# A convolution-attention kernel in float32: another way through the last pair of heads, and another order of the first loads

## The chip, the cores and the metric

The kernel runs on one core of one Trainium2 chip. The metric is the device time of one execution in microseconds (us); a profile of one execution is taken beside the timed runs. Two kinds of number are used: medians of timed runs, and moments in the profiled execution, counted from its start. In lines of a profile PE is TensorE, PEld its weight loads, DVE VectorE, ACT ScalarE, POOL GpSimd and SP SyncE, which issues most transfers; a q behind a name is that engine's queue of instructions.

## The reference, cut to what matters

Four images of 384 channels and 48 x 48 pixels go through one block: a 7 x 7 depthwise convolution is layer-normed and added to the queries of an 8-head self-attention over the 2304 pixels, followed by a projection and a residual.

```python
local = conv(x, conv_w, groups=C) * inv + (bn_beta - bn_mean * inv)     # 7x7, depthwise
x_norm = layernorm(x_flat, ln_gamma, ln_beta)
q, k, v = split(x_norm @ qkv_w.T + qkv_b)                               # 8 heads of 48
q = q + heads(layernorm(local_flat, ln_gamma, ln_beta))
attn = softmax(q @ k.T * 48 ** -0.5)
out = x_flat + (attn @ v) @ proj_w.T + proj_b
```

## The kernel before

The work is cut into 24 tiles (`t`) of 384 pixels (8 image rows); each tile goes through four pairs of heads. The sums of a pair, `pt` times `v`, carry a column of ones, so the softmax denominators arrive as row 48 of each head. Up to pair 2 a pair fills one 128-row chunk of `ao` (rows 0 to 47 and 64 to 111); the 96 rows of pair 3 are cut in six pieces that fill the gaps. The denominators go through DRAM to be inverted by 128 lanes and broadcast back. The end of the program, for the last tile:

```python
def pair_end(t, p):                       # cut
    for j in range(2):
        r = 64 * j
        nc.scalar.copy(dst[r : r + HA], sums[r : r + HA, :G])
        nc.sync.dma_start(out=den[2 * p + j : 2 * p + j + 1], in_=dst[r + HD : r + HA])
    if p == NP - 1:                       # six pieces of pair 3 into the gaps of ao
        ...

def divide(t):                            # cut
    nc.sync.dma_start(out=rd, in_=den)    # 8 x 384 sums on 128 lanes, 24 each
    nc.vector.reciprocal(rd, rd)
    nc.sync.dma_start(out=rden, in_=rd)
    # every reciprocal is checked against a safe range; the result goes into `inside`
    ...                                   # four broadcasts of rden into rb
    return rb

weigh()                                   # the last sums
load_residual(NT - 1)
rb = divide(NT - 1)
ao = outputs[NT - 1][0]
nc.vector.tensor_mul(ao, ao, rb)
for co in range(CC):
    output_step(NT - 1, co)               # project 3 chunks, add bias and residual, store
# then: count the lanes outside the range -> flag -> every engine loads the flag and
# branches: nothing more to do, or a second pass with shifted exponents
```

The start, before the first tile's scores (about 148 us), convolves the first tile partly on TensorE (the first `PE_TAPS` taps, as products with diagonal matrices that ScalarE makes) and partly on VectorE, norms the six pieces of the first image in turn ("cycles"), and folds the norm's beta into the projections' biases: three rows computed on TensorE (`row`) go to DRAM (`bias`) and come back as columns (`columns`, then `qkb`), because the kernel adds a bias as one value to a lane.

```python
load_slab(0, 0)                           # SP queue: image rows for the first convolution
...                                       # 14 vector pieces, in turn on the ACT and the SP queue
load_x(0, 0)
load_packed(w_v, ...)                     # then staged[1], x1, staged[0], x2 to x5, w_o,
...                                       # the second slab and the first residual
```

Of the kernel before, what the change touches and what calls it, by code (L numbers as in the profile page):

```python
# [16 lines left out]
NH = 8  # L17
# [9 lines left out]
OUT_SLOTS = 5, 8, 10  # L27
PE_TAPS = 12

# [13 lines left out]
def unshifted_pass(  # L43
# [94 lines left out]
    nc.sync.dma_start(out=taps_in, in_=conv_w)  # L138
    load_slab(0, 0)
    nc.gpsimd.tensor_scalar_add(inv, norms[:, 3], BN_EPS)  # L140
    nc.gpsimd.tensor_tensor(inv, inv, neg_half, ALU.pow)
# [34 lines left out]
    ]  # L176
    load_x(0, 0)
    load_packed(w_v, qkv_wT[:, 2 * C :])
# [38 lines left out]
    def conv_ops(t):  # L217
# [9 lines left out]
        for tap in taps if t else taps[PE_TAPS:]:  # L227
            for c in range(CC):
# [11 lines left out]
                yield  # L240

    def first_products(dst, c):
        slab, first, end = slabs[0, 0]
        for i, tap in enumerate(taps[:PE_TAPS]):
            n = c * PE_TAPS + i
            diagonal = diagonals[n // 6].rearrange("p i f -> p (i f)")[:, n % 6 * P :][:, :P]
            nc.scalar.mul(diagonal, ident, cw[:, c, tap : tap + 1])
            src, part = window(slab, dst, 0, first, end, c, tap)
            nc.tensor.matmul(
                part, lhsT=diagonal, rhs=src, start=i == 0, stop=i == PE_TAPS - 1  # L250
            )
# [142 lines left out]
    def weights_layout():  # L394
# [11 lines left out]
        for c in range(CC):  # L406
            nc.scalar.mul(w_v[:, c], w_v[:, c], gain[:, c : c + 1])
        for i in (1, 0):
            if i == 0:
                for j, m in enumerate(rows):  # L410
                    nc.scalar.copy(row[0:1, :, j], m)
                nc.sync.dma_start(out=bias.rearrange("(o c) i -> o c i", o=1), in_=row[0:1])
# [57 lines left out]
    def pair_end(t, p):  # L470
# [6 lines left out]
        ao, ao3, den = outputs[t]  # L477
        dst = ao[:, p, :] if p < CC else ao3
        for j in range(2):
            r = 64 * j  # L480
            nc.scalar.copy(dst[r : r + HA], sums[r : r + HA, :G])  # L481
            nc.sync.dma_start(out=den[2 * p + j : 2 * p + j + 1], in_=dst[r + HD : r + HA])
        if p == NP - 1:
            for c in range(CC):
                for r in (0, 64):
                    nc.sync.dma_start(
                        out=ao[r + HD : r + 64, c, :], in_=ao3[r + 16 * c : r + 16 * c + 16]
                    )

    def divide(t):  # L490

        ao, ao3, den = outputs[t]
        few = NH * G // P
        rd = work.tile([P, few], F32, tag="rd", name="rd")
        rden = dram.tile([NH, G], F32, tag="rden", name=f"rden{t}")
        rb = work.tile([P, CC, G], F32, tag="rb", name="rb", bufs=1)
        flat = "h (k f) -> (h k) f"
        nc.sync.dma_start(out=rd, in_=den.rearrange(flat, f=few))
        nc.vector.reciprocal(rd, rd)
        nc.sync.dma_start(out=rden.rearrange(flat, f=few), in_=rd)  # L500

        for bound, op in ((SAFE, ALU.is_le), (1 / SAFE, ALU.is_ge)):
            nc.vector.scalar_tensor_tensor(inside, rd, bound, inside, op, ALU.mult)
        heads = rden[0:6].rearrange("(c h) n -> h c n", h=2)
        for j in range(2):
            r = 64 * j
            nc.sync.dma_start(
                out=rb[r : r + HD], in_=heads[j : j + 1].to_broadcast([HD, CC, G])
            )
            last = rden[6 + j : 7 + j].rearrange("o (x n) -> o x n", x=1)  # L510
            nc.sync.dma_start(out=rb[r + HD : r + 64], in_=last.to_broadcast([16, CC, G]))
        return rb
# [11 lines left out]
    def output_step(t, co):  # L524
        b, g = divmod(t, NG)
        ao, xr = outputs[t][0], residuals[t]
        m = bank()
        project(m[:, :G], lambda c: w_o[:, c, co * P : (co + 1) * P], lambda c: ao[:, c, :])
        nc.vector.scalar_tensor_tensor(  # L529
            xr[:, co, :], m[:, :G], pb[:, co : co + 1], xr[:, co, :], ALU.add, ALU.add  # L530
        )
# [52 lines left out]
    r, r2 = ring(), ring()  # L584
    products = r[:, 0, :G], r[:, 1, :G], r2[:, 0, :G]
    first_products(products[0], 0)
    convolve_first(16)
# [18 lines left out]
    for g in range(NG):  # L606
# [12 lines left out]
        if g == NG - 1:  # L619
            r, r2 = ring(), ring()  # L620
            for u, m in enumerate((r[:, 0], r[:, 1], r2[:, 0])):
                query_step(0, u, m)
        convolve_first(6)
        rs = newton(*root)
# [9 lines left out]
    for t in range(NT):  # L634
# [14 lines left out]
        for s in range(NSLOT):  # L649
            scores(t, s)  # L650

            if s == 2 and t:
                rb = divide(t - 1)
            if s == X_SLOTS[1] + 1 and coming is not None:
                rs = newton(*root)
# [32 lines left out]
            if s == OUT_SLOTS[0] - 1 and t:  # L688
                ao = outputs[t - 1][0]
                nc.vector.tensor_mul(ao, ao, rb)  # L690
            if s == X_SLOTS[0] - 1 and coming is not None:
                total[X_SLOTS[0]] = chunk_sum(coming)
# [4 lines left out]
            if s == first + 1 and following:  # L697
                total[second] = chunk_sum(sq)
    weigh()
    load_residual(NT - 1)  # L700
    rb = divide(NT - 1)
    ao = outputs[NT - 1][0]
    nc.vector.tensor_mul(ao, ao, rb)  # L703
    for co in range(CC):
        output_step(NT - 1, co)

# [527 lines left out]
```

## Time and profile before

The median is 3159.97 us of the first three runs (3156.47 to 3162.11). The profiled span is 3159.7 us. It falls into three stretches:

| stretch | from, to (us) | length |
|---|---|---|
| start: until the first scores | 0 to 147.94 | 147.9 |
| middle: 24 tiles, TensorE never idle | 147.94 to 3127.79 | 2979.9 |
| end: behind the last sums | 3127.79 to 3159.7 | 31.9 |

First, the bias round trip in the timeline of the kernel before (columns: start us, length us, engine, line, operation, destination<-source, count; "SPq" is the queue of SyncE):

```profile
50.93 0.29 SPq L412 DMA_DIRECT2D bias<-row  x1
53.64 1.76 SPq L96 DMA_DIRECT2D columns<-bias  x4
```

The columns can be issued only when the row has landed: 53.64 less 50.93 is 2.7 us. Second, the branch at the end, in the view of its source line (engine, operation, count, shortest/median/longest ns, first and last start):

```profile
L727 POOLq COMPARE_BRANCH  x1: 62/62/62, 3137.1 to 3137.1; - x1
L727 POOLq EVENT_SEMAPHORE  x1: 17/17/17, 3141.0 to 3141.0; - x1
L727 SPq COMPARE_BRANCH  x1: 45/45/45, 3154.9 to 3154.9; - x1
L727 SPq EVENT_SEMAPHORE  x8: 17/17/17, 3157.4 to 3158.0; - x8
```

GpSimd (POOL) branches 18 us before SyncE does, since the flag is ready at 3136.5 and GpSimd has nothing else to do. The branch itself takes 62 ns, but its next instruction starts 3.9 us later; for SyncE it is 2.5 us.

### The profile page before, as it was taken

To read this page: it belongs to the slowest core of one execution; us is meant where nothing else is said; L and a number is where in the kernel's file an instruction comes from. 1 tells how busy PE (TensorE), PEld (TensorE's weight loads), DVE (VectorE), ACT (ScalarE), POOL (GpSimd) and SP (SyncE) were. 2 spreads that over 40 slices of the span, in tenths; PEclk is the share of its full clock that TensorE was granted. 3 is DMA by queue.
4 is the path that set the end of the run, shared out by engine and by line. 5 is a ranking of instruction groups with operands and counts; after the bars stand their busy time and mean duration, and the time that the engine had idled before them with its cause. 6 is when DMAs were issued, how large, how long until landed. Compare 5 with 4: busy or idle time off the path is not lost.

```text
span 3159.7 us, 41999 instructions
## 1 busy us (share of the span) xinstructions
PE 3074.7 (97%) x15854; PEld 1375.8 (44%) x15854; DVE 2189.8 (69%) x4184; ACT 1615.3 (51%) x2395; POOL 13.1 (0%) x49
## 2 busy tenths in 40 slices
PE   7999999999999999999999999999999999999997
PEld 3544444444454444444454444444445444444443
DVE  6899878867717788778681878877757287777310
ACT  4455555555445555555534555555552555555552
POOL 1000000000000000000000000000000000000000
PEclk9999999999999999999999999999999999999998
DMA  6111111011101111111111111012011001100001
GB/s 110 32 22 28 33 24 43 25 28 37 29 23 31 34 32 28 33 30 31 29 36 24 26 30 43 25 24 45 25 20 30 18 25 31 26 22 20 14 25 32
DMA packets 77255, 96.51 MB, mean 31 GB/s; under 512 B 22193, under 2 KB 67825, under 8 KB 77042
## 3 DMA queue, kind: packets, MB, share of 16 engines
q1 hardware_dynamic: 76322, 93.68, 13.1%
q8 instruction: 127, 2.08, 0.3%
q14 instruction: 86, 0.70, 0.1%
q10 hardware_dynamic: 304, 0.04, 0.0%
q0 software_dynamic: 416, 0.01, 0.0%
HBM read 68.22 MB, written 14.75 MB: 26 GB/s over the span
## 4 chain that ended last, share of the span: by engine, by line
PE 90%; ACT 5%; DMA 2%; DVE 1%; issue 1%; SPq 0%; POOL 0%; ACTq 0%; DVEq 0%
PE r L551 36%; PE o L564 35%; PE m L342 10%; PE r L342 7%; PE m L313 3%; ACT pt L555 2%; ACT u L328 1%; ACT y L329 1%; ACT u L330 1%; ACT sq L321 1%; DVE acc L239 0%; ACT ao L481 0%; DMA xn<-in_x_dram 0%; DMA staged<-in_qkv_wT_dram 0%; DVE xn L626 0%
## 5 line engine op out<-in xcount | busy, mean ns | idle before, releaser
L555 ACT ACTIVATE pt<-r 128x768 f32<-128x768 f32 x1728 | 1275.8, 811 | 1161.0 <-PE o L564 889.1
L239 DVE SCALAR_TENSOR_TENSOR acc<-slab,vec,acc 128x360 f32<-128x360 f32 (+3 forms) x3423 | 1733.5, 588 | 8.1 <-POOL acc L225 7.6
L564 PE MATMUL o<-pt,v 128*49 128x384 f32 x6912 | 1175.5, 490 | 0.0
L551 PE MATMUL r<-q,k 48*128 48x384 f32 x5184 | 920.3, 500 | 6.1 <-ACT pt L555 6.1
L564 PEld LDWEIGHTS o<-pt,v 128*49 128x49 f32 x6912 | 426.3, 124 | 710.0 <-issue 710.0
L551 PEld LDWEIGHTS r<-q,k 48*128 48x128 f32 x5184 | 434.0, 185 | 491.1 <-ACT pt L555 251.2
L551 PE MATMUL r<-qt,kt 48*128 48x384 f32 x1728 | 309.1, 499 | 29.7 <-ACT pt L555 29.7
L529 DVE SCALAR_TENSOR_TENSOR xr<-m,pb,xr 128x384 f32<-128x384 f32 x72 | 44.5, 618 | 298.2 <-PE m L342 298.2
L551 PEld LDWEIGHTS r<-qt,kt 48*128 48x128 f32 x1728 | 147.9, 185 | 189.8 <-ACT pt L555 108.7
L317 DVE TENSOR_TENSOR xn<-xn,m 128x1152 f32<-128x1152 f32 x24 | 32.5, 1354 | 254.1 <-PE m L313 254.1
L342 PE MATMUL m<-ao,w_o 128*128 128x384 f32 x432 | 164.7, 519 | 8.6 <-DVE ao L703 7.2
L342 PE MATMUL m<-xn,w_qk 128*128 128x384 f32 x414 | 152.0, 503 | 0.0
L342 PE MATMUL r<-xn,w_qk 128*128 128x384 f32 x450 | 149.3, 486 | 0.7 <-ACT q L454 0.7
L342 PE MATMUL r<-w_v,xn 128*128 128x384 f32 x432 | 145.3, 489 | 0.0
L334 DVE SCALAR_TENSOR_TENSOR u<-m,eps,u 128x384 f32<-128x384 f32 x48 | 29.6, 618 | 130.0 <-ACT u L330 129.8
L342 PEld LDWEIGHTS m<-ao,w_o 128*128 128x128 f32 x432 | 79.0, 196 | 89.9 <-issue 38.1
L342 PEld LDWEIGHTS r<-xn,w_qk 128*128 128x128 f32 x450 | 85.4, 190 | 60.6 <-ACT q L454 1.3
L342 PEld LDWEIGHTS r<-w_v,xn 128*128 128x128 f32 x432 | 82.4, 191 | 59.0 <-issue 3.0
L342 PEld LDWEIGHTS m<-xn,w_qk 128*128 128x128 f32 x414 | 73.0, 189 | 74.2 <-issue 27.8
L481 ACT COPY ao<-o 49x384 f32<-49x384 f32 x144 | 68.3, 474 | 68.7 <-PE o L564 66.9
L313 PE MATMUL m<-sum,mean_w 128*128 128x384 f32 x192 | 88.0, 540 | 10.5 <-DVE sum L307 8.5
L382 ACT COPY v<-r 128x384 f32<-128x384 f32 x72 | 32.2, 482 | 126.8 <-PE r L342 126.8
(78 smaller groups left out, 741.1 us busy)
## 6 DMA issues: line engine op xcount, KB each, us to landing
xr<-in_x_dram SPq DMA_DIRECT2D x24, 576.0 KB
out_dram<-xr SPq DMA_DIRECT2D x72, 192.0 KB
slab<-in_x_dram SPq DMA_DIRECT2D x32, 378.0 KB
xn<-in_x_dram SPq DMA_DIRECT2D x48, 216.0 KB
rb<-rden SPq DMA_DIRECT2D x48, 216.0 KB
slab<-in_x_dram SPq DMA_DIRECT2D x16, 297.0 KB
slab<-in_x_dram SPq DMA_DIRECT2D x32, 126.0 KB
xn<-in_x_dram SPq DMA_DIRECT2D x48, 72.0 KB
```

What stands on the lines that cost most here:

```text
L239: nc.vector.scalar_tensor_tensor(dst, src, weight, dst, ALU.mult, ALU.add)
L313: nc.tensor.matmul(m[:, :G], lhsT=mean_w, rhs=s, start=True, stop=True)
L317: nc.vector.tensor_sub(src, src, over_chunks(m[:, :G]))
L321: nc.scalar.activation(sq, src, AF.Square)
L328: nc.scalar.activation(u, m[:, :G], AF.Ln, bias=eps)
L342: nc.tensor.matmul(dst, lhsT=weights(c), rhs=src(c), start=c == 0, stop=c == CC - 1)
L382: nc.scalar.copy(v[:, u + NB, :, 0:HD], r[:, j, :C].rearrange("p (h d) -> p h d", d=HD))
L481: nc.scalar.copy(dst[r : r + HA], sums[r : r + HA, :G])
L529: nc.vector.scalar_tensor_tensor(xr[:, co, :], m[:, :G], pb[:, co : co + 1], xr[:, co, :], ALU.add, ALU.add)
L551: nc.tensor.matmul(r[:, j, :G], lhsT=kk[:, blk * P : (blk + 1) * P], rhs=qq, start=True, stop=True)
L555: nc.scalar.activation(pt, r[:, :, :G], AF.Exp, scale=SCALE)
L564: nc.tensor.matmul(sums[r : r + HA, :G], lhsT=values[t // NG, kb // NB][:, kb % NB, 2 * p + j, :], rhs=pt[:, j, :], start=kb == 0, stop=kb ...
```

## The change

At the end, six heads of the last tile are divided before the last pair is done; the sums of heads 6 and 7 are spread over their lanes by a small product, inverted where they lie and projected from where they lie with a weight tile of their own, so that nothing of the last pair goes through DRAM on the path. At the start, the first x is loaded ahead of the vectors, all diagonals are made first, two taps move from TensorE to VectorE, and one bias row is copied early.

```diff
-PE_TAPS = 12
+PE_TAPS = 10
     load_slab(0, 0)
+    load_x(0, 0)
 ...                                                   # vectors
-    load_x(0, 0)
     load_packed(w_v, qkv_wT[:, 2 * C :])
 ...
+    make_diagonals()                                  # was: inside first_products, set by set
     first_products(products[0], 0)
 ...
+        nc.scalar.copy(row[0:1, :, 2], rows[2])       # ahead of the scaling of the weights
         for i in (1, 0):
             if i == 0:
-                for j, m in enumerate(rows):
-                    nc.scalar.copy(row[0:1, :, j], m)
+                for j in (1, 0):
+                    nc.scalar.copy(row[0:1, :, j], rows[j])
 ...
-        convolve_first(6)
+        convolve_first(7)
 ...
+            if s == NSLOT - 1 and not following:      # last slot of the last tile
+                load_residual(t)
+                rb = divide(t, 6)                     # heads 0 to 5
 ...
     weigh()
-    load_residual(NT - 1)
-    rb = divide(NT - 1)
-    nc.vector.tensor_mul(ao, ao, rb)
-    for co in range(CC):
-        output_step(NT - 1, co)
+    r, r2 = ring(), ring()
+    parts = r[:, 0, :G], r[:, 1, :G], r2[:, 0, :G]
+    first_six(0)                                      # 3 products of chunk 0, not yet closed
+    m = bank()
+    nc.tensor.matmul(m[:, :G], lhsT=ending[:, 1, 0:P], rhs=ao3, start=True, stop=True)
+    for co in range(1, CC):
+        first_six(co)
+    nc.vector.reciprocal(y, m[:, :G])
+    nc.vector.tensor_mul(ao3, ao3, y)
+    for co in range(CC):
+        nc.tensor.matmul(parts[co], lhsT=ending[:, 0, co * P : (co + 1) * P], rhs=ao3,
+                         start=False, stop=True)
+        finish(NT - 1, co, parts[co])                 # bias, residual, store
+    reciprocals(NT - 1, 6, NH)                        # the check of heads 6 and 7
```

(Cut: the two copies of the last pair on two engines, the fill of `ending`, the memsets.)

More of the change, by code (lines that the diff above doesn't have):

```diff
@@ L240, in conv_ops, with diagonal, make_diagonals @@
                 yield
+    def diagonal(c, i):
+        n = c * PE_TAPS + i
+        return diagonals[n // 6].rearrange("p i f -> p (i f)")[:, n % 6 * P : n % 6 * P + P]
+    def make_diagonals():
+        for c in range(CC):
+            for i, tap in enumerate(taps[:PE_TAPS]):
+                nc.scalar.mul(diagonal(c, i), ident, cw[:, c, tap : tap + 1])
     def first_products(dst, c):
@@ L244, in first_products @@
         for i, tap in enumerate(taps[:PE_TAPS]):
-            n = c * PE_TAPS + i
-            diagonal = diagonals[n // 6].rearrange("p i f -> p (i f)")[:, n % 6 * P :][:, :P]
-            nc.scalar.mul(diagonal, ident, cw[:, c, tap : tap + 1])
             src, part = window(slab, dst, 0, first, end, c, tap)
             nc.tensor.matmul(
-                part, lhsT=diagonal, rhs=src, start=i == 0, stop=i == PE_TAPS - 1
+                part, lhsT=diagonal(c, i), rhs=src, start=i == 0, stop=i == PE_TAPS - 1
             )
@@ L478, in pair_end @@
         dst = ao[:, p, :] if p < CC else ao3
+        final = t == NT - 1
+        if final and p == 0:
+            nc.gpsimd.memset(ao, 0.0)
+            nc.gpsimd.memset(ao3, 0.0)
         for j in range(2):
             r = 64 * j
-            nc.scalar.copy(dst[r : r + HA], sums[r : r + HA, :G])
+            if final and j:
+                nc.vector.tensor_copy(dst[r : r + HA], sums[r : r + HA, :G])
+            else:
+                nc.scalar.copy(dst[r : r + HA], sums[r : r + HA, :G])
             nc.sync.dma_start(out=den[2 * p + j : 2 * p + j + 1], in_=dst[r + HD : r + HA])
-        if p == NP - 1:
+        if p == NP - 1 and not final:
             for c in range(CC):
@@ L488, in pair_end, with reciprocals, divide @@
                     )
-    def divide(t):
-        ao, ao3, den = outputs[t]
+    def reciprocals(t, h0, h1):
         few = NH * G // P
-        rd = work.tile([P, few], F32, tag="rd", name="rd")
-        rden = dram.tile([NH, G], F32, tag="rden", name=f"rden{t}")
-        rb = work.tile([P, CC, G], F32, tag="rb", name="rb", bufs=1)
-        flat = "h (k f) -> (h k) f"
-        nc.sync.dma_start(out=rd, in_=den.rearrange(flat, f=few))
-        nc.vector.reciprocal(rd, rd)
-        nc.sync.dma_start(out=rden.rearrange(flat, f=few), in_=rd)
-        for bound, op in ((SAFE, ALU.is_le), (1 / SAFE, ALU.is_ge)):
-            nc.vector.scalar_tensor_tensor(inside, rd, bound, inside, op, ALU.mult)
+        n = (h1 - h0) * G // few
+        rd = work.tile([P, few], F32, tag="rd", name="rd")[0:n]
+        nc.sync.dma_start(
+            out=rd, in_=outputs[t][2][h0:h1].rearrange("h (k f) -> (h k) f", f=few)
+        )
+        nc.vector.reciprocal(rd, rd)
+        for bound, op in ((SAFE, ALU.is_le), (1 / SAFE, ALU.is_ge)):
+            nc.vector.scalar_tensor_tensor(inside[0:n], rd, bound, inside[0:n], op, ALU.mult)
+        return rd
+    def divide(t, n=NH):
+        rb = work.tile([P, CC, G], F32, tag="rb", name="rb", bufs=1)
+        rden = dram.tile([NH, G], F32, tag="rden", name=f"rden{t}")
+        if n < NH:
+            nc.gpsimd.memset(rb, 0.0)
+        rd = reciprocals(t, 0, n)
+        nc.sync.dma_start(
+            out=rden[0:n].rearrange("h (k f) -> (h k) f", f=NH * G // P), in_=rd
+        )
         heads = rden[0:6].rearrange("(c h) n -> h c n", h=2)
@@ L509, in divide @@
             )
-            last = rden[6 + j : 7 + j].rearrange("o (x n) -> o x n", x=1)
-            nc.sync.dma_start(out=rb[r + HD : r + 64], in_=last.to_broadcast([16, CC, G]))
+            if n == NH:
+                last = rden[6 + j : 7 + j].rearrange("o (x n) -> o x n", x=1)
+                nc.sync.dma_start(out=rb[r + HD : r + 64], in_=last.to_broadcast([16, CC, G]))
         return rb
@@ L524, in output_step, with finish @@
     def output_step(t, co):
-        b, g = divmod(t, NG)
-        ao, xr = outputs[t][0], residuals[t]
+        ao = outputs[t][0]
         m = bank()
         project(m[:, :G], lambda c: w_o[:, c, co * P : (co + 1) * P], lambda c: ao[:, c, :])
+        finish(t, co, m[:, :G])
+    def finish(t, co, m):
+        b, g = divmod(t, NG)
+        xr = residuals[t]
         nc.vector.scalar_tensor_tensor(
-            xr[:, co, :], m[:, :G], pb[:, co : co + 1], xr[:, co, :], ALU.add, ALU.add
+            xr[:, co, :], m, pb[:, co : co + 1], xr[:, co, :], ALU.add, ALU.add
         )
@@ L653, in unshifted_pass @@
                 rb = divide(t - 1)
+            if s == 0 and not following:
+                ending = big.tile([P, CC, G], F32, tag="xn0", name="ending")
+                nc.gpsimd.memset(ending[:, 0, :], 0.0)
+                for j in range(2):
+                    r = 64 * j
+                    nc.sync.dma_start(
+                        out=ending[r : r + HD, 0, :], in_=proj_wT[(6 + j) * HD : (7 + j) * HD]
+                    )
+                    nc.gpsimd.tensor_copy(
+                        ending[:, 1, r : r + 64], ident[:, r + HD : r + HA].to_broadcast([P, 64])
+                    )
+            if s == NSLOT - 1 and not following:
+                load_residual(t)
+                rb = divide(t, 6)
             if s == X_SLOTS[1] + 1 and coming is not None:
@@ L690, in unshifted_pass @@
                 nc.vector.tensor_mul(ao, ao, rb)
+            if s == NSLOT - 1 and not following:
+                ao = outputs[t][0]
+                nc.vector.tensor_mul(ao, ao, rb)
             if s == X_SLOTS[0] - 1 and coming is not None:
@@ L699, in unshifted_pass, with first_six @@
     weigh()
-    load_residual(NT - 1)
-    rb = divide(NT - 1)
-    ao = outputs[NT - 1][0]
-    nc.vector.tensor_mul(ao, ao, rb)
-    for co in range(CC):
-        output_step(NT - 1, co)
+    ao, ao3, _ = outputs[NT - 1]
+    r, r2 = ring(), ring()
+    parts = r[:, 0, :G], r[:, 1, :G], r2[:, 0, :G]
+    def first_six(co):
+        for c in range(CC):
+            nc.tensor.matmul(
+                parts[co],
+                lhsT=w_o[:, c, co * P : (co + 1) * P],
+                rhs=ao[:, c, :],
+                start=c == 0,
+                stop=False,
+            )
+    first_six(0)
[3 more added lines that the diff above has]
+        first_six(co)
+    y = work.tile([P, G], F32, tag="y", name="y", bufs=1)
+    nc.vector.reciprocal(y, m[:, :G])
+    nc.vector.tensor_mul(ao3, ao3, y)
+    for co in range(CC):
+        nc.tensor.matmul(
+            parts[co],
+            lhsT=ending[:, 0, co * P : (co + 1) * P],
+            rhs=ao3,
+            start=False,
+            stop=True,
+        )
+        finish(NT - 1, co, parts[co])
+    reciprocals(NT - 1, 6, NH)
 def conv_attention(tc: tile.TileContext, *args):
```

## The prediction

> **What bounds the kernel now.** I read the page first (busy shares, chain), then the timeline and chain of waits of the last 60 us and the first 150 us, because the listing of both kernels' instruction orders shows that between the first and the last of the 24 tiles nothing moves on any engine.
>
> ```profile
> PE 3074.7 (97%) x15854; PEld 1375.8 (44%) x15854; DVE 2189.8 (69%) x4184; ACT 1615.3 (51%) x2395; POOL 13.1 (0%) x49
> PE 90%; ACT 5%; DMA 2%; DVE 1%; issue 1%; SPq 0%; POOL 0%; ACTq 0%; DVEq 0%
> ```
>
> Busy shares, then the chain by engine: from about 148 us to 3128 us TensorE is never without a matmul, and the change touches none of those. It can only win at the two ends: some 148 us at the start and 32 us at the end. The chain of waits at the end (start us, us, what):
>
> ```profile
> 3119.89 7.90 PE o L564 x48
> 3127.82 0.47 ACT aot L481
> ...
> 3128.32 0.48 ACT aot L481
> ...
> 3132.92 1.73 DMA rd<-den
> ...
> 3135.00 1.43 DMA rden<-rd
> ...
> 3137.78 3.81 DMA rb<-rden
> ...
> 3141.77 1.37 DVE ao L703
> ...
> 3143.18 4.22 PE m L342 x6
> ...
> 3148.11 2.22 PE m L342 x6
> ...
> 3153.26 0.62 DVE xr L529
> ```
>
> After the last sums (3127.8) come two copies, eight small transfers, three dependent transfers through DRAM, one product, and three projections in turn through one PSUM bank: 26.1 us to the last DVE end at 3153.9, then 5.8 us of output transfer, flag load, branch and program end to 3159.7. The start, from the timeline (start, busy, engine, line, what):
>
> ```profile
> 8.84 4.75 SPq L160 DMA_DIRECT2D vec<-natural  x7
> 12.40 7.13 ACT L247 ACTIVATE pt<-ident,vec 128x128 f32<-128x128 f32 x24 [10.37 <-DMA vec<-natural]
> 34.04 9.27 PE L249 MATMUL r<-slab,pt 128*128 128x384 f32 x24 [2.13 <-ACT pt L247]
> 50.95 0.91 PE L313 MATMUL m<-sum,mean_w 128*128 128x384 f32 x2 [1.75 <-ACT row L411]
> 57.11 0.23 DVE L426 TENSOR_TENSOR qkb<-qk_vec,columns 128x3 f32<-128x3 f32 x2 [2.49 <-DMA columns<-bias]
> 83.99 0.91 PE L313 MATMUL m<-sum,mean_w 128*128 128x384 f32 x2 [1.17 <-DVE sum L307]
> ```
>
> The weight vectors gate ScalarE's diagonals; the third set of diagonals stands behind the root on ScalarE, so TensorE waits 2.13 us; the row products then run to 49.2, the row copies to 50.9, and DVE idles 2.49 us until the bias columns have gone through DRAM. From 57 us five cycles of about 14.6 us follow in which DVE is on the path (TensorE waits for the sum).
>
> **What the skill says.** "TensorE: Matmul & The Clock Gate", What's actually happening: after an idle window of about 3.4 us the array drops to half clock. The trace agrees: after 15 us with almost no work the first projection took 4.21 us for 6 passes, the next 2.20. "VectorE: DVE Perf Modes", First, the fixed hardware budget: Reciprocal repeats its divide step 8 times. The trace has only 128x24: 303 ns against 178 for a plain operation of that size, so about 5 ns per element beyond the usual one cycle, somewhat under 8 cycles in all. "DMA: Bandwidth & Descriptors", Issuing engines are not separate DMA queues: transfers of all issuers interleave on the same 16 engines. So a load put ahead of the vectors shares with them; the trace shows the start saturated at about 189 GB/s from 20 to 40 us.
>
> **The end, part by part** (on the time line of before).
>
> *Six heads ahead.* Pair 2's sums end at 3105.4. Their reading back is on SP directly behind their writing, but DVE takes the reciprocal only after slot 10's output step (3111.8 + 0.6). Then 0.3 reciprocal, 1.4 to DRAM, 0.4 for the residual's issue, about 4 to 6 for the two broadcasts beside the 0.59 MB residual: about 3121, and the product of 1.36 is over by 3123, before the last sums at 3127.8. Free.
>
> *Last pair.* TensorE goes on at once: 6 passes of the first projection (2.0 us at the 0.325 us a pass of the 48 sums), while ScalarE and DVE copy one head each (0.47, was 0.97 in turn). Then 2 passes spread the sums: over at 3130.5. Reciprocal of 128x384: by difference 384 x 6 ns plus 0.15 = 2.5 us, by the skill's 8 steps at its 0.96 GHz 3.2 + 0.15 = 3.35; I take 3.3 (estimates), then the product, 0.56: 3134.5. Meanwhile 12 passes of the other two projections occupy TensorE until 3134.4: even. Then three pairs of passes, 0.65 each, into three separate banks, with the 0.62 additions behind them: 3135.2 for the first pair, last DVE end 3137.2. Before: 3153.9, so 16.7 us less. The warm clock is part of it: 2 us.
>
> *Tail.* The check of heads 6 and 7 now stands behind the last addition. Before, reciprocal to flag took 3134.67 to 3136.46, 1.8 us, beside the broadcasts. Now it is on the path, since all five engines load the flag and branch at the end. Before, SP loaded it after its last issue at 3154.25 and the program ended 5.45 later. So 3137.2 + 1.8 + 5.45 = 3144.5, against 3159.7: end gain 15.2. The three outputs leave within 1.3 us; 0.59 MB at 189 GB/s is 3.1 us, landed near 3141, not later than the branch path. I take 15.
>
> **The start.** Two taps of three chunks go from TensorE to DVE: 6 matmuls of 2 passes less, 6 operations of about 0.47 us more, one in each of six cycles.
>
> *Vectors later.* The first x takes SP places ahead of the seven vector issues. Its first waits for the slab (8.84), the third for a vector of the ACT queue (10.5), so the vectors issue from about 11.6 instead of 8.84, and the last ends near 15.7, not 13.6: about +2.2 us for the first diagonals and the first full round of DVE taps (14.93 to about 17.1).
>
> *Products earlier.* DVE's 16 taps end at 24.0, the sum at 25.1 (22.9 before). Second products 20 x 0.314 = 6.3 from 26.0: 32.3; mean 0.8; third products need no new diagonals: 33.1 to 39.4, before 43.3. Eighteen row passes, 6.1 us, end at 45.5 (before 49.2). ScalarE copies one row early, scales twelve pieces (3.35) and copies two rows: about 48.6, before 50.9. The bias round trip (6.2 us) follows: columns near 54.7, before 57.0. DVE waits for them whatever else is early: gain 2.3, although the LayerNorm mean itself comes 4 to 5 us earlier (its bank is freed by the row copied early).
>
> *Cycles.* The seventh tap operation stands where DVE waits for the root. Idle there in cycles 0 to 4 was 0.5, 0.1, 0.1, 0.3, 0.5 (timeline of DVE), so of 5 x 0.47 = 2.3 some 1.3 is absorbed: +1.0. In the sixth cycle TensorE is the path. Start: 2.3 - 1.0 = 1.3 gained.
>
> **Sum.** 15.0 + 1.3 = 16.3; 3160.0 - 16.3 = 3143.7, so 3144 us, 0.5% less.
>
> **Rivals.** (1) The start loses: x0's 0.59 MB takes 3.1 us of the queue just when the vectors pass; if they queue behind all of it, first diagonals come 4 us late and the start costs 1 to 2 us: 3147. For it: the issue waits above. Against: pieces 1 and 2 fall into the idle queue between 9 and 13 us, and third diagonals and shorter products repay about 4. (2) The columns are less bound than I think and the early mean counts in full: start gain 4 to 5, 3140. Against: DVE's wait of 2.49 us for them already. (3) The tail turns into the bound: all engines fetch branch targets together after a late flag, instead of ACT and POOL at 3136.5; +2 to 3 us, 3146. For it: instruction transfers until 3158 in the last 5 us. (4) The broadcasts of the six heads are late behind the residual: the first projection waits. Against: 5 us of slack. It would make 3148. (5) A drift of the granted clock (0.91 in some stretches, 0.994 on the mean): runs of before spread 5.7 us.
>
> **Range and chances.** The end is worked from durations in the trace, give or take 2.5; the start give or take 2.5; medians give or take 2.5. Together about 4.5, so 3138 to 3150 for 8 in 10. 2% is 63 us, more than both ends' recoverable idle; a loss of 2% would need a break in the middle, where the order is equal: faster 0.01, same 0.985, slower 0.005.
>
> **What would show it.** Right: last DVE addition 9 to 10 us after the last sums instead of 26; 128x384 reciprocal 2.5 to 3.4 us; no idle over 0.5 us on TensorE between the last sums and the last projection, at full clock; flag chain of 1.8 us behind the last addition and then 5 to 6 us; first diagonal near 14.6; third products without a wait for ScalarE; bias columns near 54.7; cycles near 14.8. Wrong: first scores later than 148; the ahead product not done at 3127; an end over 8 us behind the last addition; any change in the middle's 2980 us.

## The result, and the profile after

The changed kernel is correct and takes 3149.26 us (median of six runs, 3143.74 to 3152.3), against 3160.72 of before (3156.47 to 3165.78). The ratio is 0.9962, 95% interval 0.9949 to 0.9975. Ratios here are the mean time of one kernel's fast runs over that of the other's fast runs of the same rounds, so not quite the ratio of the medians. The time lies inside the predicted range of 3138 to 3150, at its upper edge, 5 us above the point; three of the six runs lie above 3150.

The profiled span is 3149.3 us, 10.4 less. By stretch:

| stretch | before | after | gain | predicted gain |
|---|---|---|---|---|
| start | 147.94 | 149.48 | -1.5 | +1.3 |
| middle | 2979.85 | 2979.91 | -0.1 | 0 |
| end | 31.9 | 19.9 | +12.0 | +15.2 (15 taken) |

That the two middles agree to 0.1 us is chance: other profiles, below, differ there by up to 12 us.

The busy shares and the chain by engine of the changed kernel:

```profile
PE 3070.4 (97%) x15850; PEld 1374.1 (44%) x15850; DVE 2198.2 (70%) x4199; ACT 1610.6 (51%) x2385; POOL 33.1 (1%) x55
PE 91%; ACT 5%; DVE 2%; issue 1%; DMA 1%; SPq 0%; POOL 0%; ACTq 0%; DVEq 0%
```

Transfers have half their former share of the chain (1% instead of 2%), and POOL has 20 us more work (the memsets of the new ending); the rest differs by a point at most, because both ends together are under 6% of the span. The chain of waits at the end:

```profile
3129.39 2.13 PE r L756 x6
3131.52 0.65 PE m L766 x2
3132.17 3.87 PE r L756 x12
3136.04 0.66 PE r L773 x2
...
3136.72 0.63 DVE xr L558
...
3137.39 1.57 PE r L773 x4
...
3141.02 0.14 DVE flag L801
```

No transfer is left in it. TensorE works on from 3129.39 to 3136.70 without a gap; the last addition ends at 3139.60, which is 10.2 us behind the sums, where it was 26.1. Then comes the check of the last two heads, 1.56 us until the flag at 3141.16; and then, though nothing is computed any more, 8.1 us to the end. The view of the branch's line says where they are:

```profile
L803 SPq COMPARE_BRANCH  x1: 50/50/50, 3141.7 to 3141.7; - x1
L803 SPq EVENT_SEMAPHORE  x8: 17/17/17, 3145.5 to 3146.0; - x8
L803 POOLq COMPARE_BRANCH  x1: 62/62/62, 3141.8 to 3141.8; - x1
L803 POOLq EVENT_SEMAPHORE  x1: 17/17/17, 3145.6 to 3145.6; - x1
```

All engines branch within 0.1 us of each other. SyncE needs 3.8 us to its next instruction instead of 2.5, and GpSimd, which used to do this more than 18 us before the end, now does it at the same time. The last source line of the program, in the changed kernel (L1306) and in the kernel before (L1230), shows a second place:

```profile
L1306 POOLq EVENT_SEMAPHORE_RANGE_CLEAR  x1: 178/178/178, 3147.2 to 3147.2; - x1
L1306 POOLq DRAIN  x3: 107/194/1134, 3145.7 to 3148.8; - x3
L1230 POOLq EVENT_SEMAPHORE_RANGE_CLEAR  x1: 178/178/178, 3159.2 to 3159.2; - x1
L1230 POOLq DRAIN  x3: 46/107/1134, 3141.1 to 3159.4; - x3
```

From GpSimd's clearing of the semaphores to its last drain pass 1.6 us instead of 0.2. These two, 1.3 and 1.4 us, are what the tail is longer by (8.1 against 5.45 us). GpSimd's long drain of 1134 ns, which used to be over 17 us before the end, now ends at 3146.8, just before SyncE's own next step at 3146.9; that it lies on the path is not shown.

The start, in the timeline of the changed kernel:

```profile
16.45 8.88 ACT L249 ACTIVATE pt<-ident,vec 128x128 f32<-128x128 f32 x30 [14.42 <-DMA vec<-natural]
47.42 0.29 SPq L419 DMA_DIRECT2D bias<-row  x1
54.45 1.76 SPq L96 DMA_DIRECT2D columns<-bias  x4
57.52 0.23 DVE L433 TENSOR_TENSOR qkb<-qk_vec,columns 128x3 f32<-128x3 f32 x2 [7.97 <-DMA columns<-bias]
```

The diagonals start 4.05 us later than before (16.45 against 12.40), yet the row is ready 3.5 us earlier (47.42 against 50.93). But it takes 7.0 us to land instead of 2.7, and the bracket in the fourth line shows what became of the lead: VectorE sits idle for 7.97 us waiting for the columns, where it had waited 2.49. Two windows of that stretch (columns: window, its length, busy us of TensorE, its weight loads, VectorE, ScalarE, GpSimd, then TensorE's clock, the DMA engines' share and GB/s):

```profile
47.00:50.00 3.00, 3.00 (x10) 1.74 (x10) 2.55 (x4) 3.00 (x12) 0.00 (x0) 1.00 1.08 174
53.00:56.00 3.00, 0.00 (x0) 0.00 (x0) 0.00 (x0) 0.00 (x0) 0.00 (x0) 0.50 0.87 197
```

The DMA engines are still full (a share of 1.08, then 0.87) with the 8.5 MB of first loads, until about 55 us. At 47 us three engines compute, at 53 none does; TensorE's clock has dropped to 0.50, and the next mean takes 1.62 us for its two passes, as it did in the kernel before; at full clock such a mean takes 0.9.

### The profile page after: what moved, and what is told of

It is laid out like the page before. It is cut to its first block, busy times and chain, and to the rows that moved or that the text cites. A ratio compares the mean times of both kernels' runs of the same rounds, so it can differ in the third digit from the quotient of the medians.

```text
span 3149.3 us, 42010 instructions
## 1 busy us (share of the span) xinstructions
PE 3070.4 (97%) x15850; PEld 1374.1 (44%) x15850; DVE 2198.2 (70%) x4199; ACT 1610.6 (51%) x2385; POOL 33.1 (1%) x55
## 4 chain that ended last, share of the span: by engine, by line
PE 91%; ACT 5%; DVE 2%; issue 1%; DMA 1%; SPq 0%; POOL 0%; ACTq 0%; DVEq 0%
PE r L580 36%; PE o L593 35%; PE m L348 10%; PE r L348 7%; PE m L319 2%; ACT pt L584 2%; DVE acc L239 1%; ACT u L334 1%; ACT y L335 1%; ACT u L336 1%; ACT sq L327 1%; ACT ao L495 0%; PE r L255 0%; DMA bias<-row 0%; DMA vec<-natural 0%
## 5 line engine op out<-in xcount | busy, mean ns | idle before, releaser
L239 DVE SCALAR_TENSOR_TENSOR acc<-slab,vec,acc 128x368 f32<-128x368 f32 (+8 forms) x3429 | 1735.9, 583 | 11.4 <-DMA vec<-natural 11.4
L348 PE MATMUL m<-ao,w_o 128*128 128x384 f32 x414 | 155.9, 514 | 0.0
```

The costliest lines, as they stand in the source:

```text
L239: nc.vector.scalar_tensor_tensor(dst, src, weight, dst, ALU.mult, ALU.add)
L348: nc.tensor.matmul(dst, lhsT=weights(c), rhs=src(c), start=c == 0, stop=c == CC - 1)
```

## The experiments

Three questions: which end gave what; why the row took 7 us; what the tail of 8 us is made of. "First scores" is the end of the start stretch; "end stretch" is from the end of the last sums to the end of the program. The middle, whose order no kernel changes (the new ending divides its six heads in the last 25 us of it, beside a busy TensorE), was 2974.9 to 2986.9 us long in the profiles. Its length follows the clock that was granted within it: the mean over windows of 20 us from 160 to 3100 us was 0.9994 in the four shortest, 0.9976 in the profiles of before and of the changed kernel, 0.9951 in the longest. One execution may therefore differ from another by up to 12 us without any cause in the two ends, and the readings below rest on the stretches, with the times as a second witness. Each is one profiled execution.

The stretches scatter too. The same new ending stands in six profiles (the changed kernel, e1, e4, e6, e12, e13): its end stretch was 18.8 to 20.1 us long, 19.6 on the mean. The old ending, in three, took 31.9 (before), 31.4 (e17) and 34.0 us (e2, where the second projection took 4.22 us like the first, and not 2.22). Their means differ by 12.9 us, so the 12.0 of the one pair above is not far off, but a part of about 1 us inside the end can't be read from one pair.

**e1_end_only: the new ending with the old start.**

```diff
 # the changed kernel with the start of before
-PE_TAPS = 10
+PE_TAPS = 12
-        convolve_first(7)
+        convolve_first(6)
-    load_x(0, 0)                          # ahead of the vectors
+    load_x(0, 0)                          # behind the vectors
-    make_diagonals()
+            nc.scalar.mul(diagonal(c, i), ident, cw[:, c, tap : tap + 1])   # in first_products
-        nc.scalar.copy(row[0:1, :, 2], rows[2])
+                for j, m in enumerate(rows):
+                    nc.scalar.copy(row[0:1, :, j], m)
```

> The kernel before with the new ending alone (start as before: 12 taps, x loaded behind the vectors, diagonals and row copies in the old order). My theory: the two ends are independent and the ending is worth the change from 31.9 to 19.9 us between the end of the last sums and the end of the program, so first scores at 147.9 us, tail 19.9 us, and about 12.0 us less than before (3148.5). Rival: the new start had also helped and the ending is worth only 10 us or less.

Measured: 3147.64 us (3145.44 to 3148.2), ratio 0.996 [0.9947, 0.9973]; first scores at 148.55, end stretch 3143.4 - 3124.65 = 18.8 us (19.9 expected; the scatter above). The ending alone gives all that the whole change gives.

**e2_start_only: the new start with the old ending.**

```diff
 # the kernel before with the start of the change: the same five edits the other way round
-PE_TAPS = 12
+PE_TAPS = 10
 ...
```

> The kernel before with the new start alone (10 taps, first x ahead of the vectors, all diagonals first, one row copied early). My theory: the start loses; first scores at 149.5 instead of 147.9 us, tail 31.9 us, so about 1.5 us more than before, inside the scatter of the runs. Rival: what I had predicted, 1.3 us less.

Measured: 3160.18 us (3154.08 to 3167.44), ratio 0.9999 [0.9984, 1.0014]; first scores at 150.05, 2.1 later than before; the row issued at 47.09, landed at 54.00; end stretch 34.0 us, 2.1 longer than expected. The start is no gain in time and a loss in the trace.

**e4_bias_pool: the row and the columns on GpSimd's queue.** My first theory was an order on SyncE's queue: the row's transfer would stand behind the queued loads and the residual issued right behind it.

```diff
-nc.sync.dma_start(out=bias, in_=row[0:1])
+nc.gpsimd.dma_start(out=bias, in_=row[0:1])
-load_packed(columns, bias)
+load_packed(columns, bias, nc.gpsimd)
```

> The changed kernel with the bias row and the bias columns sent from GpSimd's queue instead of SP's. My theory: the bias transfer waits in SP's queue behind the weights, slab and residual issued before and after it, so on another queue it lands within 3 us of its issue near 47.5 instead of 7 us, the columns are there near 54 or before (57.5 now), and first scores come 3 to 5 us earlier, near 145 to 146.5. Rival: all 16 engines are full with loads until 55 us, so any transfer takes 7 us whatever its queue, and first scores stay at 149.5.

Measured: 3151.84 us (3144.05 to 3155.84), ratio 0.9969 [0.9954, 0.9984]; first scores at 149.22. From its timeline:

```profile
53.38 2.24 POOL L96 DMA_DIRECT2D columns<-bias  x4 [6.04 <-DMA bias<-row]
```

Issued at 46.82 on an empty queue, the row still landed only at 53.38. This theory's number fell: another queue brought nothing. That fits the Trainium skill, "DMA: Bandwidth & Descriptors", Issuing engines are not separate DMA queues: whoever issues a transfer, it runs on the same 16 engines among the others. The run does not prove it, for two reasons. The first loads were through at 51 us (from 51 to 53 the engines were 1% busy), so the last 2.4 us of the row's wait are not theirs; the columns took 1.8 to 1.9 us each on this queue with idle engines. And the first residual, issued at 47.76 in the changed kernel, was issued only at 102.39 here.

**e12_late_loads: the loads that are not needed yet, behind the columns.** The new theory: it is the engines that are full, so take load away from them. The second slab (1 MB), `w_o` and the first residual (0.6 MB each) are needed only after 120 us.

```diff
-    load_packed(w_o, proj_wT)            # among the first loads; likewise the second slab
 ...
         if g == 0:
             bias_columns()
+        if g == 1:
+            load_slab(0, 1)
+        if g == 2:
+            load_packed(w_o, proj_wT)
+            load_residual(0)
 # SP kept in program order from the bias row up to here
```

> After, with the loads that are not needed in the first 57 us (second slab, w_o, first residual: 2.2 MB) issued behind the bias columns. Theory (the bias row's transfer took 7 us because its 16 engines still held loads): the row issued at 47.4 lands in under 3 us, the columns are issued near 50, DVE's qkb near 52.5 instead of 57.5, and the first scores come 3 to 5 us earlier than after's 149.5, near 145.5; end unchanged, about 3145 us. Rival (the row's path is slow for a reason of its own, or the next chain, the squares of ScalarE and the mean, ends just behind): qkb may come earlier but first scores stay at 148.5 or later.

Measured: 3144.74 us (3140.65 to 3145.97), ratio 0.9949 [0.9936, 0.9962]; first scores at 143.01, 6.5 us before those of the changed kernel. From its timeline, and one of its windows:

```profile
47.01 0.29 SPq L421 DMA_DIRECT2D bias<-row  x1
48.25 1.74 SPq L96 DMA_DIRECT2D columns<-bias  x4
51.52 0.23 DVE L435 TENSOR_TENSOR qkb<-qk_vec,columns 128x3 f32<-128x3 f32 x2 [2.36 <-DMA columns<-bias]
```

```profile
47.00:50.00 3.00, 3.00 (x10) 1.52 (x8) 2.16 (x4) 3.00 (x12) 0.00 (x0) 1.00 0.04 2
```

The same row, issued at the same time to engines that are 4% busy, lands in 1.24 us instead of 7.03. The theory holds: the loads are the cause. The gain is larger than I expected (3 to 5) because qkb comes 6.0 us earlier, not 5; the other 0.5 us goes with TensorE's clock, which held (the mean took 0.89 us, not 1.62). The edit takes the loads out of the engines and out of SyncE's queue alike, so it does not say for which of the two the row had waited. In the changed kernel the row landed at 54.45, while the engines moved the residual that was issued behind it (329 GB/s from 54.5 to 55); so it seems to have waited for the loads issued before it, not for those behind. Whether another queue than GpSimd's would have let it pass them was not tried.

**e13_late_x_back: late loads, and the first x behind the vectors again.**

```diff
     load_slab(0, 0)
-    load_x(0, 0)
 ...                                      # vectors
+    load_x(0, 0)
     load_packed(w_v, qkv_wT[:, 2 * C :])
```

> The same late loads, and the first x loaded behind the vectors again as in before. Theory (x ahead made the vectors 3 us late, and that lies on the path once the columns no longer wait for the stream): first diagonal near 12.4, bias row issued near 45, qkb near 50.5, first scores 1 to 2 us before those of the run with late loads alone. Rival: the first x then comes later and the mean waits for it, or the stream of loads still holds the engines at 45 us: first scores equal within 0.5 us.

Measured: 3137.96 us (3135.86 to 3149.15), ratio 0.9936 [0.9922, 0.9951]; row issued at 44.37, qkb at 48.82, first scores at 140.31. That is 2.70 us before e12, and the two kernels differ in nothing else: so much, in one profile of each, the first x ahead of the vectors costs once the loads are late. The times of the two are not told apart by their intervals.

**e6_x_back: the same edit on the changed kernel, loads as they were.**

> After with the first x loaded behind the vectors again, loads otherwise as in after. Theory (the columns are bound by the stream of loads, not by the work before them): first diagonal near 12.4, bias row issued near 44.5, but it still lands near 54, qkb near 57, first scores 148.5 to 149.5, time as after. Rival (the vectors' delay is what the start lost): row lands 3 us earlier and first scores come near 146.5.

Measured: 3145.73 us (3143.36 to 3155.14), ratio 0.9951 [0.9937, 0.9964]; row issued at 44.16, landed at 50.94 (6.8 us), first scores at 146.39. The rival's numbers came, not the theory's. Only half of the theory stands: the row took 6.8 us to land behind full engines. The moment at which the engines come free is no constant. In this execution they moved 197 GB/s between 22 and 40 us, in the profile of the changed kernel 178. These are 0.34 MB more in 18 us, worth about 1.8 us at 190 GB/s (an estimate from these rates), of the 3.5 us by which the row landed earlier than in the changed kernel. So this pair does not separate the place of the first x from the rate of the stream, and whether the place acts on the rate stays open. e4_bias_pool does not help: its rate was 195 and its loads were through at 51 us, when the row landed here, but its own row, on GpSimd's queue, landed 2.4 us later. The price of the first x rests on e13_late_x_back alone.

**e17_before_late: the kernel before with late loads.** The edit is that of e12_late_loads.

> Before with late loads only. Its bias row is issued at 50.9, when the loads are nearly through, so by my theory it gains at most 1 us: row landed by 53, qkb 56 to 57, first scores 147 to 148, time within 2 us of before. Rival: the loads also slow something else in the start (the cycles' own loads and gathers), and before gains as much as after does, 3 us or more.

Measured: 3155.03 us (3153.73 to 3160.42), ratio 0.9991 [0.9979, 1.0004]; row issued at 50.86, landed at 52.10, qkb at 55.40, first scores at 145.64. In the trace 2.3 us earlier than before, over the 1 us that I allowed, under the rival's 3. With the loads out of the way in both, the whole start of the change is worth 145.64 - 143.01 = 2.6 us, and without the first x's move 145.64 - 140.31 = 5.3. The products' early end was a real gain; the loads hid it.

**e11_flag_early: the check before the last two additions, and three PSUM tiles for the three products.**

```diff
-    r, r2 = ring(), ring()
-    parts = r[:, 0, :G], r[:, 1, :G], r2[:, 0, :G]
+    parts = [ring()[:, 0, :G] for _ in range(CC)]
 ...
     nc.vector.tensor_mul(ao3, ao3, y)
+    reciprocals(NT - 1, 6, NH)
+    nc.vector.tensor_scalar(outside, inside, 0.5, None, ALU.is_lt)
 ...                                      # count behind the first product,
 ...                                      # flag behind the first addition
-    reciprocals(NT - 1, 6, NH)           # and the chain to the flag behind the pass
```

> The changed kernel with the check of heads 6 and 7, its count and the flag made behind the first of the last three additions instead of behind the last, and the three projections in three separate ring buffers. My theory: the tail grew because with the late flag all five engines load the flag and branch at the same moment, and GpSimd's branch and drain come onto the path; with the flag about 2 to 3 us earlier the program ends 5.5 to 6.5 us after the last addition instead of 9.7, and the second projection no longer waits for the first addition (0.7 us less), so 4 to 5 us less than the changed kernel, tail from the last sums about 15.5. Rival: the end is bound by the outputs' landing or by the program's end itself, and only the 0.7 us come.

Measured: 3148.21 us (3144.01 to 3151.51), ratio 0.9959 [0.9946, 0.9971]; end stretch 3149.5 - 3132.98 = 16.5 us instead of 19.9. From its chain of waits:

```profile
3139.63 0.65 PE r L777 x2
3140.28 0.14 PE m L785 x2
3140.41 1.50 PE r L777 x4
```

The second product follows without the 0.7 us that it waited in the changed kernel, where it writes the other half of a PSUM tile that the first addition still reads. 3.4 us are gained in the trace; in the time it does not show: first scores came at 149.82, and the middle was 2983.2 us long in this profile, 3.3 more than in that of the changed kernel. I had expected 15.5; the flag, at 3141.18, still comes late: GpSimd branches at 3141.8, SyncE 1.7 us behind it, and SyncE then needs 3.3 us to its next instruction.

**e18_flag_six: the flag made from six heads, right behind the last sums.** It leaves the check of the last two heads out on purpose; the outputs are the same.

```diff
     rb = divide(t, 6)
+    nc.vector.tensor_scalar(outside, inside, 0.5, None, ALU.is_lt)
 ...
+    nc.tensor.matmul(count, lhsT=ones, rhs=outside, start=True, stop=True)
+    nc.vector.tensor_reduce(total, count, AX.X, ALU.add)
+    nc.vector.tensor_copy(flag, total)
     first_six(0)
 ...
-    reciprocals(NT - 1, 6, NH)
```

> After, with the flag made from six heads of the last pair's tile just after the last sums and the last two heads left unchecked (so the check of this data is incomplete on purpose; the outputs are the same). Theory (a late flag lets all five engines branch at once, and then each needs 3.6 to 4.1 us to go on, where engines that branch apart need about 2.5): the check chain of 1.56 us goes, ScalarE and GpSimd branch near 2 us after the last sums, the last addition comes 10.2 us after the sums as in after, and the end 5.5 to 6 us behind it: 15.5 to 16 us from the last sums to the end instead of 19.9. Rival (a branch costs 3.6 to 4.1 us whenever it is taken, and GpSimd's drain is always on the path): only the chain goes, 18 us or more.

Measured: 3143.66 us (3142.87 to 3148.69), ratio 0.9945 [0.9931, 0.9958]; end stretch 3144.7 - 3127.79 = 16.9 us. The branch's line:

```profile
L803 POOLq COMPARE_BRANCH  x1: 62/62/62, 3129.9 to 3129.9; - x1
L803 SPq COMPARE_BRANCH  x1: 45/45/45, 3139.4 to 3139.4; - x1
L803 SPq EVENT_SEMAPHORE  x8: 17/17/17, 3142.0 to 3142.6; - x8
```

The last addition is again 10.4 us behind the sums, but GpSimd has branched long before, and SyncE needs 2.6 us to its next instruction, not 3.8. Of the 3.0 us gained, 0.7 come because SyncE branches 11.6 us behind the sums instead of 12.3 (the check chain of 1.56 us is gone, but SyncE still has the outputs to issue), 1.2 because it goes on 2.6 us after its branch instead of 3.8, and 1.1 lie between GpSimd's clearing of the semaphores and its last drain (0.5 instead of 1.6 us). The 1.2 us are the late flag's: SyncE took 3.7 to 4.2 us in the six profiles of the new ending, in which all engines branch together, and 2.5 to 2.7 in the three of the old. The 1.1 are not shown to be: that interval was 0.2 to 1.7 us long in the same six profiles. The theory had asked for 15.5 to 16 and the rival for 18 or more; the result lies between, nearer to the theory, since SyncE branches only 1.25 us behind the last addition, when it has issued the outputs. By chance this profile shows the start at its worst: the stream moved 165 GB/s, the row landed at 57.43, first scores at 152.87.

**e15_best_x_back: what the experiments point to.** Late loads, first x behind the vectors, and the ending of e11_flag_early.

> A version meant to beat both: the new ending with three PSUM tiles and the check made before the last two additions, late loads, first x behind the vectors. Start as in the run with late loads and x back (first scores near 144), end as in the run with the early check (16.5 us from the last sums to the end): 3141 us. If gains at the two ends do not add: 3144 or more.

Measured: 3134.94 us (3133.55 to 3140.23), ratio 0.9925 [0.9912, 0.9938]: 25 us under before, 14 under the changed kernel's median (of other rounds), 6 under what I expected, and correct. First scores at 140.72 (144 expected), end stretch 3131.6 - 3115.78 = 15.8 us (16.5 expected). Against the profile of before that is 7.2 at the start and 16.1 at the end; the remaining 4.8 of the span lie in the untouched middle (2975.1 us; the clock granted in it was 0.9994, against 0.9976 in before) and are not this version's merit.

**e16_best_end_start12: the same with 12 taps on TensorE and six operations a cycle.**

```diff
-PE_TAPS = 10
+PE_TAPS = 12
-        convolve_first(7)
+        convolve_first(6)
```

> The best version so far with 12 taps on TensorE and six tap operations in a cycle, as in before. Theory (the seventh operation costs 1 us over the cycles, the two further taps cost 6 x 0.65 us of TensorE and 6 diagonals of ScalarE before the columns): qkb 1 to 2 us later than 48.76, cycles 1 us shorter: first scores within 1 us of 140.7, time within 2 us of 3135. Rival (the taps' shift is worth what was meant): first scores 2 us or more later, near 143.

Measured: 3141.69 us (3139.23 to 3143.86), ratio 0.9935 [0.9922, 0.9949]; qkb at 50.91, its second mean at 52.66, first scores at 141.17. The columns come 2.15 us later than in e15 and the cycles from that mean to the first scores take 88.5 us instead of 90.2: the shift of two taps is nearly a draw, 0.45 us in this pair. Some 0.5 us of that is chance: the mean took 1.62 us in e15 and 0.88 here, and at full clock seven operations took 89.7 us (e12, e13), so with equal clocks the 12 taps lose about 0.9. The theory holds for the first scores, its columns came a little later than it allowed (1 to 2 us), and its time, within 2 us of 3135, was missed by nearly 7; the middle was 6.6 us longer than in e15. The times, taken in different rounds, do not tell the two apart.

## Why the prediction was right or wrong

**The total** (3144, measured 3149) is inside the range, and the largest term, the ending without transfers, is right: e1_end_only has all of the gain. Two terms were wrong, both on the same side, and each by more than the 2.5 us that the prediction gave it: the start by 2.8, the end by 3. That the sum stayed in the range is owed to the range's width. Two of its four signs of being wrong came: first scores later than 148 (149.48), and an end over 8 us behind the last addition (9.7).

**Six heads ahead; TensorE at work through the end.** Right. The product of the six heads was started at 3123.1 and over at 3124.4, 5 us before the last sums ended; spread over at 2.8 us behind them (predicted 2.7), at full clock.

**Reciprocal of 128x384.** I took 3.3 us; it was 2.56, and my estimate by difference (2.5) was the better one. It did not matter: the twelve passes beside it ended 6.65 us behind the sums (the sum had 6.6), and the product that waits for the reciprocal before them, at 5.97. (A pass of 0.325 us is 7.90 us over 24 pairs of sums, not over 48; the passes of the ending took 0.32 to 0.36.)

**Last addition.** Predicted 9.4 us behind the sums, measured 10.2. "Three pairs of passes into three separate banks" was the step: two of the three parts share one PSUM tile, and the second product waited 0.7 us for the first addition. e11_flag_early takes that wait away. The two head copies, meant to run side by side on two engines, ran one after the other, 1.07 us together; this was hidden.

**Check chain.** Predicted 1.8, measured 1.56: right.

**Tail.** "The program ended 5.45 later" was the step that failed: I carried the time behind SyncE's last issue over from a program in which the flag was already 18 us old. Measured 8.1 us behind the flag, and 7.0 to 8.3 in the six profiles of this ending. This is rival 3 by its size of 2 to 3 us. Half of it is shown to be the late flag's: SyncE goes on 3.8 us after its branch, where it took 2.5, and e18_flag_six, with an early flag, brings it back to 2.6. The other 1.4 us, between GpSimd's last clearing of semaphores and its last drain, were 0.2 to 1.7 us long with the same ending; their cause is open, and part of them may be chance. That the engines hinder one another in fetching what follows the branch is argued from this, not shown. Together: 0.8 for the additions, -0.2 for the check, 2.7 for the tail are, but for rounding, the 3.2 us between 15.2 and 12.0.

**Vectors later.** Predicted 2.2 us, and 14.6 for the first diagonal; measured 4.05 and 16.45 (full rounds of VectorE: 3.0). e13_late_x_back puts its price on the path at 2.7 us. Rival 1 had the 4 us of the diagonals and the amount, a start that loses 1 to 2 us, but not the way: in spite of the late diagonals the row was ready 3.5 us earlier, and the start was lost behind it.

**Products earlier.** Right, and even better than worked out: no wait of the third products, row issued at 47.42 (predicted 48.6).

**"The bias round trip (6.2 us) follows: columns near 54.7."** This step failed. 6.2 us was a duration measured in the kernel before, where the row was issued at the end of the load stream; moved 3.5 us earlier it stood behind loads under way, and took 10.1 us from issue to qkb. I had noted the saturation from 20 to 40 us and did not ask when it ends. e12_late_loads shows that the loads are the cause. Whether the row waits for full engines or for its turn in SyncE's queue is not separated; e4_bias_pool shows only that GpSimd's queue is no way around them.

**Cycles.** Predicted +1.0 us. From the second mean of the first cycle to the first scores: 90.2 after against 89.1 before. One pair would prove little, but the nine profiles with seven operations average 90.2 and the four with six 89.1 (88.5 to 90.1). Right.

## What to carry to other kernels

A duration of a small transfer belongs to the loads that are under way at that moment: before work in front of it is pulled earlier, look up whether they are still running there, and put loads that are needed later behind it. A wait that is shortened at the end of a program can hand its time on to what was hidden beside it, here a check and a branch; count what else will start late. Where two ends change, measure them by stretches of the trace, for a drift of the clock in an untouched middle can be as large as the gain.

## What the Trainium skill lacked or had wrong

- "DMA: Bandwidth & Descriptors", Anatomy of one DMA, gives a fixed cost of about 2.0 us per transfer for the GpSimd path. The row of 4.5 KB, issued by SyncE, landed in 1.24 us on idle engines (e12_late_loads, e13_late_x_back, e17_before_late) and in 7.0 us behind the first loads; issued by GpSimd beside these loads it took 6.6 us, the last 2.4 with idle engines, while the columns took 1.8 to 1.9 us on GpSimd's queue, near the page's figure. What a small transfer costs behind a full stream, in numbers, is lacking there.
- "Advanced Engine Details and Errata", Control Flow Timing, gives about 108 ns for a compare-and-branch. The instruction took 45 to 72 ns on four engines, but the next instruction came 2.5 to 4.4 us later on every one of them, and on TensorE the branch itself shows 3.4 to 5.0 us. What it costs to go on after a branch is given a time on no page; "Runtime: NRT & Kernel Launch", Instruction fetch mechanics, speaks of a stall after a taken branch, without a figure.
- "VectorE: DVE Perf Modes", First, the fixed hardware budget, has the reciprocal's 8 repeats but no time. The 128x384 reciprocal took 2.56 us; less 0.15 us for the instruction (a plain operation of 24 elements took 178 ns) that is 6.3 ns an element (an estimate from these runs).
- No page that I read gives the spread of the rate at which first loads stream in: between 22 and 40 us it was 165 to 197 GB/s in the profiles of these kernels. With the same start, 178 GB/s went with first scores at 149.48 (the changed kernel) and 165 with 152.87 (e18_flag_six).
